# A graph layer's edge stages in a fixed order, its features and its router's ranks in batches

## The chip, the cores and the metric

The kernel runs on one core of one Trainium2 chip. The core has five engines with an instruction queue each: TensorE (PE, matrix products), VectorE (DVE), ScalarE (ACT), GpSimd (POOL; here it issues the indirect gathers) and SyncE (SP; here it only issues transfers). Each engine takes its instructions in order; they wait for each other by semaphores. The metric is device microseconds of one execution, the median of several.

## The reference

3125 nodes of 256 features and 53,125 edges (25,000 both ways, and one loop per node) pass four blocks, each added to its input after a layer norm. The names of the kernel's stages follow them.

```python
x = x + gnn0(layernorm(x), edge_index, edge_weight, ...)   # attention of four heads over the edges
x = x + moe0(layernorm(x), ...)                            # 16 experts, the best two of each node
x = x + gnn1(layernorm(x), src, dst, edge_type, ...)       # relations: 200 kinds of edges
x = x + ffn1(layernorm(x), ...)                            # only the rows with the highest router weight

# gnn0, per head:  w = exp(-relu((a_s[src] + a_d[dst] + aw_e * elem + ab) / 20))
#                  out = segment_sum(w * feats[dst], src) / segment_sum(w, src)
# gnn1:            alpha = exp(leaky_relu(h[src].w_src + h[dst].w_dst + rel_e.w_rel)); alpha / sum over its one column
#                  agg = segment_sum((h[src] + rel_e) @ Wn * alpha, dst); out = relu(agg) + loop_message
# ffn1:            weights = x @ wr + br; the kk best rows of each batch: gelu(x @ w1 + b1) @ w2 + b2, times weight
```

## The kernel before

The nodes stand in SBUF as 25 tiles of 128 rows (`self.x`). The edges of each graph layer are sorted on the chip by the node tile that receives them, so that each node tile is a bucket of 18 (the last has 8) edge tiles of 128 edges, 440 edge tiles in all. Up to six edge tiles make a group (`GRP`), which gives 74 groups in a layer.

The stages follow one another: the sort of layer 0's edges and layer 0's features; layer 0's edges (`heads_edges`); the experts and the combine of their results (`experts`); norms and features for layer 1 (`relations_features`); layer 1's edges (`relations_edges`); router and FFN (`depths`). The sort of layer 1's edges runs underneath: a generator `ranking` yields pieces of work that the edge loop of layer 0 draws one by one (`fill`), and its `move` steps run among the experts' row tiles.

For a group of edges the loop does this. GpSimd gathers a row of the feature table for each edge (L754, one indirect DMA per edge tile, into one of three `rows` buffers). SP loads the edges' other end, spread over all partitions, as `wide` (L744, one load per bucket, per kind of spread; layer 0 has one kind, layer 1 two). VectorE compares: `oh` (L762) is the one-hot of each edge's receiving node, `hot` (L771) that of the near rows as columns (one in layer 0, three in layer 1). TensorE multiplies `hot` with the near values into `ps_near` (L780), VectorE reduces it to `near` (L787). The weights follow: in layer 0 three VectorE steps `s` (L919 to L921) and two exponentials on ScalarE (L924, L925), then the message `rows` times weight (L926); in layer 1 `s` (L1310, L1279), the exponential (L1280), `s` again (L1281, L1282), a one-hot of the relation written behind the gathered row (L1313), and on ScalarE the one-hot of the node times the weight, `ohw` (L1319). TensorE adds it all up in PSUM, `ps_sums` (L798), over the tiles of a bucket. At a bucket's end VectorE adds what lay beyond the bucket's tiles, `more` (L804, a load on SP), giving `acc` (L806), and a `finish` function turns it into the node tile's new `x`. In layer 0 that also runs the gate in batches of node tiles (`gate`: norms, the experts' logits); in layer 1 it runs relation and loop products (`ps_rel`, `ps_loop`).

The order of these is only half written: `edge_stages` returns three stages, `gather` (with the comparisons), `message` and `add`, and `pipelined` calls them for groups one behind the other. The program runs under a scheduler, which places the instructions of each engine by its own estimates; that is the order in each queue.

After the experts, the combine gathers two result rows per node (L1170) and adds them to `x` (L1174). `relations_features` then loads its weights (`w3a`, `av`, L1198), takes their product (L1203), normalises all 25 tiles with one square root over them (`layer_norm("xn2")`, L157 to L163), and for each tile transposes it (`ps_x_t`), multiplies it by the weights (`ps_f`, L1264), copies it out and writes the table (L1270, five tiles a write).

`depths` starts behind layer 1's edges: weights loaded (L1375 on), all norms, the router weight of each row (`junk`, L1396, with `wc` as sums), a row of all weights on each partition (`wrow`, L1406 and L1410), and then the rank of each row as a count: for each of 25 tiles a comparison with all of `wrow` (`cmp`, L1426, in two pieces around the tile itself) and one for ties (`eq`, L1431). Rows whose rank is under `kk` get their weight as factor, and the FFN runs four tiles at a time (`ps_hid` L1453, `ps_out` L1464).

## Time and profile before

| | us |
|---|---|
| median of 3 runs (lowest to highest) | 2857.28 (2856.35 to 2861.86) |
| the profiled execution | 2845.15 |
| its span | 2842.8 |
| mean granted TensorE clock | 0.822 |

| engine | busy us | share of the span |
|---|---|---|
| TensorE | 1878.6 | 66% |
| VectorE | 1446.3 | 51% |
| GpSimd | 1167.4 | 41% |
| ScalarE | 390.7 | 14% |

The profile counts the busy time of each engine, and for the groups of instructions of one line the idle time of the engine in front of them, with the instruction that ended it. "issue" means that the engine waited for nothing that the profile shows, "remote" that what it waited for is not in the trace. The shares are means over stages with different limits; a stretch of the span has to be read by itself. Line numbers are those of the kernel printed above.

### The profile page before, as it was taken

Reading aid. Unit: us, or ns where it says so; the run is one execution under the profiler, and the core shown is the slowest. Engines: PE = TensorE matmul, PEld = TensorE weight load, DVE = VectorE, ACT = ScalarE, POOL = GpSimd, SP = SyncE. Lnnn points to the kernel's source line nnn. Section 1 sums busy time; section 2 is a strip of 40 time slices with the busy share of each in tenths; the row PEclk is TensorE's granted clock in tenths of the full one; section 3 lists DMA queues with packets and bytes.
Section 4 is the critical chain, followed back from the end, with each engine's and each line's share of the span. In section 5 each row is a group of like instructions: output and inputs, shape, how many; then the busy total and the mean of one; then the engine's idle time right before and its main releaser. Section 6 shows DMA issues by size and latency. Waiting matters only on the chain.

```text
span 2842.8 us, 24381 instructions
## 1 busy us (share of the span) xinstructions
PE 1878.6 (66%) x7534; PEld 1126.4 (40%) x7534; DVE 1446.3 (51%) x3397; ACT 390.7 (14%) x1097; POOL 1167.4 (41%) x1198
## 2 busy tenths in 40 slices
PE   3169554854544443399999991447878778785298
PEld 0024232543433332356666660323434334343166
DVE  4876225476665343644422224445655556549721
ACT  0000010010000000100112120112222222221012
POOL 4235306576654646034411115036666666650000
PEclk9999996676666667577799996768889888898599
DMA  2000325343444433144499982254545455431000
GB/s 83 0 3 5 104 89 137 93 130 112 115 100 114 116 100 101 49 150 130 131 316 318 317 291 84 87 156 131 148 129 148 130 142 149 128 85 34 8 21 18
DMA packets 258938, 334.04 MB, mean 118 GB/s; under 512 B 30861, under 2 KB 192407, under 8 KB 258807
## 3 DMA queue, kind: packets, MB, share of 16 engines
q1 hardware_dynamic: 197527, 191.26, 21.3%
q0 software_dynamic: 51920, 132.68, 17.6%
q10 hardware_dynamic: 9360, 8.52, 0.9%
q8 instruction: 61, 1.00, 0.1%
q14 instruction: 70, 0.57, 0.1%
HBM read 298.38 MB, written 33.98 MB: 117 GB/s over the span
## 4 chain that ended last, share of the span: by engine, by line
PE 39%; DVE 14%; issue 10%; POOL 9%; another core or an unknown queue 8%; DMA 4%; ACT 1%; SPq 0%; DVEq 0%; POOLq 0%; ACTq 0%
PE ps_sums L798 10%; PE ps_h L1130 9%; POOL rows L754 9%; PE ps_y L1147 4%; PE s_mv L560 3%; DVE cmp L1426 3%; PE ps_hid L1453 3%; PE ps_out L1464 3%; DMA rows<-table,s_idx 3%; DVE msg L926 2%; DVE hot L771 2%; PE ps_x_t L173 1%; PE ps_h_t L173 1%; PE ps_f L1264 1%
## 5 line engine op out<-in xcount | busy, mean ns | idle before, releaser
L754 POOL DMA_INDIRECT rows<-table,s_idx x880 | 848.6, 964 | 725.0 <-issue 240.4
L798 PE MATMUL ps_sums<-msg,oh 128*128 128x260 f32 x880 | 306.6, 519 | 261.8 <-DVE msg L926 143.1
L798 PE MATMUL ps_sums<-rows,ohw 128*128 128x457 f32 x880 | 414.0, 616 | 62.8 <-ACT ohw L1319 54.1
L798 PEld LDWEIGHTS ps_sums<-msg,oh 128*128 128x128 f32 x880 | 226.6, 265 | 325.1 <-issue 250.1
L560 PE MATMUL s_mv<-s_hv,s_hp 128*128 128x200 f16 (+1 forms) x832 | 246.8, 472 | 89.9 <-DVE s_hv L555 89.9
L798 PEld LDWEIGHTS ps_sums<-rows,ohw 128*128 128x128 f32 x880 | 179.0, 215 | 217.5 <-issue 149.6
L1130 PE MATMUL ps_h<-w,x_t 128*128 128x512 f32 x520 | 256.1, 638 | 0.0
L771 DVE TENSOR_SCALAR hot<-wide,pcols 128x768 bf16<-128x768 bf16 (+1 forms) x296 | 175.4, 597 | 73.9 <-PE ps_near L780 63.0
L560 PEld LDWEIGHTS <-s_hp 128*128 128x128 f16 x832 | 122.1, 147 | 208.7 <-issue 180.3
L762 DVE TENSOR_TENSOR oh<-ps_hold,s_row 128x768 f32<-128x768 f32 (+1 forms) x148 | 139.9, 946 | 125.7 <-remote 73.5
L1119 POOL DMA_INDIRECT xg<-xtab,who x65 | 61.9, 952 | 345.1 <-PE ps_x_t L173 302.6
L569 POOL DMA_INDIRECT s_tab<-s_rec,s_to x130 | 147.8, 1137 | 115.1 <-ACT s_rec L566 78.9
L780 PEld LDWEIGHTS <-hot 128*128 128x128 bf16 x1760 | 70.0, 98 | 212.3 <-issue 149.2
L1136 DVE TENSOR_TENSOR hid<-hid,ps_h 128x512 f32<-128x512 f32 x65 | 44.7, 688 | 210.3 <-ACT hid L1135 204.4
L1319 ACT ACTIVATE ohw<-oh,s 128x128 f32<-128x128 f32 x440 | 136.5, 388 | 106.6 <-DVE s L1282 75.2
L1130 PEld LDWEIGHTS ps_h<-w,x_t 128*128 128x128 f32 x520 | 102.8, 209 | 105.7 <-issue 105.5
L926 DVE TENSOR_TENSOR msg<-rows,ps_hold 128x1536 f32<-128x1536 f32 x74 | 128.1, 1731 | 2.0 <-ACT ps_hold L924 1.9
L787 DVE TENSOR_REDUCE near<-ps_near 128x24 f32<-128x72 f32 (+2 forms) x148 | 29.4, 198 | 190.3 <-remote 150.2
L1147 PE MATMUL ps_y<-w,h_t 128*128 128x256 f32 x520 | 122.9, 379 | 0.7 <-ACT h_t L175 0.7
L1147 PEld LDWEIGHTS ps_y<-w,h_t 128*128 128x128 f32 x520 | 98.7, 190 | 41.7 <-issue 30.6
L545 DVE TENSOR_TENSOR s_hp<-num_p,s_pp 128x1024 f16<-128x1024 f16 x104 | 71.8, 690 | 82.8 <-PE s_mv L560 81.4
L1313 DVE TENSOR_TENSOR rows<-ps_hold,s_val 128x1200 f32<-128x1200 f32 x74 | 101.1, 1367 | 6.1 <-PE ps_sums L798 6.1
(307 smaller groups left out, 2344.2 us busy)
## 6 DMA issues: line engine op xcount, KB each, us to landing
w<-in_L_ffn_w_dram SPq DMA_DIRECT2D x195, 512.0 KB
wide<-s_w SPq DMA_DIRECT2D x72, 576.0 KB
rows<-table,s_idx POOLq DMA_INDIRECT x880
ytab<-y ACTq DMA_DIRECT2D x65, 128.0 KB
sums<-sums_z SPq DMA_DIRECT2D x5, 1142.5 KB
more<-sums SPq DMA_DIRECT2D x25, 228.5 KB
sums<-sums_z SPq DMA_DIRECT2D x5, 650.0 KB
table<-f SPq DMA_DIRECT2D x5, 650.0 KB
```

Source lines behind the costliest of these rows:

```text
L560: nc.tensor.matmul(ps[:, : NK * V], hp[:, :, j], rec[:, :, :, j].rearrange("p k v -> p (k v)"), start=(j0 + j == 0), stop=(j0 + j == C - 1),)
L569: d = nc.gpsimd.indirect_dma_start(out=tab, out_offset=bass.IndirectOffsetOnAxis(ap=to[:, i : i + 1], axis=0), in_=out[:, k * CH * V : (k ...
L754: nc.gpsimd.indirect_dma_start(out=rows[:, j, :width], out_offset=None, in_=table, in_offset=bass.IndirectOffsetOnAxis(ap=st["idx"][:, k + ...
L762: nc.vector.tensor_tensor(oh[:, :n, :], numbers[:, None, :P].to_broadcast(sh), st["row"][:, k : k + n, None].to_broadcast(sh), op=OP.is_equal,
L771: nc.vector.tensor_scalar(t[:, : n // 2, :], w, at, None, op0=OP.is_equal)
L798: nc.tensor.matmul(ps[:, :W], oh[:, j, :], msg[:, j, :], start=(head and j == 0), stop=(last and j == n - 1),)
L926: nc.vector.tensor_tensor(msg[:, :n, :HO].rearrange("p j (h o) -> p j h o", o=O), rows[:, :n, :HO].rearrange("p j (h o) -> p j h o", o=O), ...
L1130: nc.tensor.matmul(ph[:, i * HID : (i + 1) * HID], xt[:, c, :], w12[:, i, c, :], start=(c == 0), stop=(c == C - 1),)
L1147: nc.tensor.matmul(py[:, :D], ht[:, c, :], w3[:, c, :], start=(c == 0), stop=(c == HC - 1))
L1313: nc.vector.tensor_tensor(rows[:, :n, R0:], self.numbers[:, None, :R].to_broadcast(sh), st["val"][:, k : k + n, None].to_broadcast(sh), op ...
L1319: nc.scalar.activation(ow[:, j, :], oh[:, j, :], AF.Copy, scale=s[:, 1, j : j + 1])
L1426: nc.vector.tensor_scalar(cmp[:, s:e], wrow[:, s:e], w, None, op0=op, op1=OP.add, accum_out=rank[:, t, i : i + 1],)
```

## The change

- Both edge stages run in an order that is written out and that the scheduler leaves alone (`edges`, under `manual_schedule`). In each step: the spread of the group two ahead (now one `wide` load per group and kind, four buffers; `more` with the bucket's first), the gathers of group g, its comparisons and its near products on TensorE, in layer 1 the relation's one-hot, then weights, message and sums of group g-1, then the near reduction of group g, one piece of `fill`, and the end of a bucket for group g-2.
- `relations_features` is a generator. Its weights are prepared before the experts; the norms and features of layer 1 follow the combine in batches of node tiles (ends 4, 8, 12, 16, 20, 22, 25).
- The router of the last block, but for the FFN itself, leaves `depths`. Its weights are loaded ahead of layer 1's edges; norms, router weights and counts run in batches in the `finish` of layer 1's edges (ends 5, 10, 15, 20, 23, 25). A batch counts its new columns for the old tiles, and all columns so far for the new ones, into further columns of `rank`; `depths` adds them up.

```diff
-    def edge_stages(self, pool, st, table, width, into, near, others, messages, W, sums, finish):
+    def edges(
+        self, pool, st, table, width, into, near, others, messages, W, sums, finish,
+        fill=(), prepare=None,
+    ):
...
+        def spread(g):
+            b, k, n = groups[g][:3]
+            wide[g] = []
+            for i, w in enumerate(st["wide"]):
+                t = pool.tile([P, G // 2, 2 * P + 8], BF16, name=f"wide{i}", bufs=4)
+                src = w[k : k + n, :].rearrange("(o k i) p -> o k (i p)", o=1, i=2)
+                nc.sync.dma_start(t[:, : n // 2, : 2 * P], src.to_broadcast([P, n // 2, 2 * P]))
+                wide[g].append(t[:, : n // 2, : 2 * P])
+            if groups[g][3]:
+                more[b] = pool.tile([P, W], F32, name="more")
+                nc.sync.dma_start(more[b], sums[b])
...
+        with tc.manual_schedule():
+            spread(0)
+            spread(1)
+            for g in range(len(groups) + 2):
+                if g + 2 < len(groups):
+                    spread(g + 2)
+                if g < len(groups):
+                    rows = gather(g)
+                    oh, pe = hots(g)
+                    if prepare:
+                        prepare(*groups[g][1:3], rows)
+                if 0 <= g - 1 < len(groups):
+                    message(g - 1)
+                if g < len(groups):
+                    live[g] = rows, oh, picked(g, pe)
+                    if g > 0:
+                        next(fill, None)
+                if 0 <= g - 2:
+                    close(g - 2)
+            for _ in fill:
+                pass
...
-    def experts(self, fill):
+    def experts(self, fill, done):
...
                         self.x[:, t, :], yg, top[i][:, t : t + 1], self.x[:, t, :],
                         op0=OP.mult, op1=OP.add,
                     )
+                done(t)
...
-            self.h1 = self.layer_norm("xn2")
+            self.h1 = self.normed("xn2")
...
+            ends = list(range(4, NT - 4, 4)) + [NT - 3, NT]
+            def done(b):
+                if b + 1 not in ends:
+                    return
+                i = ends.index(b + 1)
+                t0, t1 = ends[i - 1] if i else 0, b + 1
+                self.norm_tiles(self.h1, t0, t1)
...
+        def route(b):
+            if b + 1 not in ends:
+                return
+            i = ends.index(b + 1)
+            t0, t1 = ends[i - 1] if i else 0, b + 1
+            self.norm_tiles(z, t0, t1)
+            for t in range(t0, t1):
+                junk = pool.tile([P, D], F32, name="junk")
+                nc.vector.scalar_tensor_tensor(
+                    junk, z[:, t, :], 1.0, wr, op0=OP.mult, op1=OP.mult,
+                    accum_out=wc[:, t : t + 1],
+                )
...
+            end = min(N, t1 * P)
+            for t in range(t0):
+                count(t, t0 * P, end, OP.is_gt, 3 + i)
+            for t in range(t0, t1):
+                lo, hi = t * P, min(N, (t + 1) * P)
+                count(t, 0, lo, OP.is_ge, 0)
+                count(t, lo, end, OP.is_gt, 1)
...
-                    self.experts([lambda f=f: f(moves) for f in steps])
-        self.relations_features()
-        self.relations_edges(load())
-        self.depths()
+                    self.experts([lambda f=f: f(moves) for f in steps], next(features))
+                    next(features, None)
+        st = load()
+        with tc.tile_pool(name="route", bufs=1) as pool:
+            self.router(pool)
+            self.relations_edges(st)
+            self.depths()
```

## The prediction

> **What bounds the kernel now.** I cut the span at its stage borders first, since shares over the whole of it mix different limits. This is the busy time of each engine by stretch: layer 0's edges, experts, combine and layer 1's features, layer 1's edges, the router, the last FFN.
>
> ```profile
> core 0: us, PE busy (x) PEld busy (x) DVE busy (x) ACT busy (x) POOL busy (x), PEclk, DMA share, GB/s
> 434.00:1170.00 736.00, 384.19 (x1586) 282.81 (x1586) 406.83 (x958) 51.54 (x190) 429.28 (x437) 0.68 0.40 108
> 1170.00:1714.00 544.00, 507.55 (x1904) 320.97 (x1904) 204.75 (x447) 87.71 (x165) 131.85 (x132) 0.87 0.68 221
> 1714.00:1892.00 178.00, 46.08 (x245) 32.96 (x245) 78.18 (x219) 12.16 (x29) 63.66 (x67) 0.66 0.35 109
> 1892.00:2565.00 673.00, 528.34 (x2449) 266.08 (x2449) 372.67 (x947) 172.95 (x591) 399.92 (x424) 0.87 0.49 131
> 2565.00:2683.00 118.00, 35.68 (x139) 25.50 (x140) 115.08 (x238) 12.21 (x20) 0.25 (x1) 0.65 0.06 20
> 2683.00:2842.80 159.80, 151.81 (x562) 101.95 (x562) 30.52 (x69) 35.73 (x59) 0.00 (x0) 0.98 0.06 20
> ```
>
> Experts and the last FFN are TensorE's. The router is VectorE's alone (115 of 118 us). In the two edge stages no engine is busy throughout, so the next view is what their costly groups wait for (layer 0's stretch):
>
> ```profile
> L754 POOL DMA_INDIRECT rows<-table,s_idx x437 | 429.4, 983 | 295.2 <-DVE msg L926 161.5 <-issue 122.5 <-DVE r L937 6.7
> L762 DVE TENSOR_TENSOR oh<-ps_hold,s_row 128x768 f32<-128x768 f32 (+1 forms) x73 | 69.0, 945 | 99.2 <-remote 73.5 <-PE ps_sums L798 16.7 <-issue 9.0
> L787 DVE TENSOR_REDUCE near<-ps_near 128x24 f32<-128x72 f32 x74 | 16.8, 227 | 78.7 <-remote 38.7 <-PE ps_near L780 35.5 <-issue 4.5
> L806 DVE TENSOR_TENSOR acc<-ps_sums,more 128x260 f32<-128x260 f32 x25 | 10.6, 425 | 84.2 <-remote 70.8 <-PE ps_sums L798 10.1 <-issue 3.1
> ```
>
> A gather takes 0.95 us plus 0.30 us of issue, so one every 1.25 us: 440 of them need 550 us. The stage takes 736, and the difference of 186 is almost the waits marked "remote" (73.5 + 38.7 + 70.8 = 183), whose releaser the trace does not see. One of them, from the timeline:
>
> ```profile
> 820.40 1.75 DVE L926 TENSOR_TENSOR msg<-rows,ps_hold 128x1536 f32<-128x1536 f32 x1
> ...
> 829.85 0.94 POOL L754 DMA_INDIRECT rows<-table,s_idx  x1 [0.30 <-issue]
> 834.72 0.43 DVE L806 TENSOR_TENSOR acc<-ps_sums,more 128x260 f32<-128x260 f32 x1 [12.57 <-remote]
> 835.30 1.21 PE L798 MATMUL ps_sums<-msg,oh 128*128 128x260 f32 x2 [16.11 <-DVE acc L806]
> ```
>
> VectorE stands 12.57 us in front of the bucket's sum, TensorE stands with it, and GpSimd issues gathers until its three row buffers are full. Layer 1 has the same sight at every bucket, where its near reduction waits (105.8 us "remote" over the stage):
>
> ```profile
> 2123.09 0.18 DVE L787 TENSOR_REDUCE near<-ps_near 128x6 f32<-128x18 f32 x1 [4.54 <-remote]
> 2123.50 0.94 POOL L754 DMA_INDIRECT rows<-table,s_idx  x1 [2.80 <-PE ps_near L780]
> 2123.84 0.61 DVE L771 TENSOR_SCALAR hot<-wide,pcols 128x768 bf16<-128x768 bf16 x1
> 2124.43 0.61 DVE L771 TENSOR_SCALAR hot<-wide,pcols 128x768 bf16<-128x768 bf16 x1
> 2124.75 0.95 POOL L754 DMA_INDIRECT rows<-table,s_idx  x1 [0.30 <-issue]
> ```
>
> **The change part by part.** Sums go against the profiled execution, 2845.15 us (span 2842.8 and 2.35 outside); the median of the runs is 2857.28, so 12.1 us are added at the end.
>
> *The router leaves the tail.* Before, 118 us lie between the last edge result (2565) and the last FFN (2683): 25 normalisations 8.2 us, 25 junk products 8.7, 49 comparisons 88.9, 25 ties 7.8, small reads 8.9, and starts. After, five batches of five, five, five, five and three tiles run inside layer 1's edges; two tiles remain. For these: two normalisations and products about 3 us, transposes and the copy about 2, 23 short comparisons of 181 columns (2 tiles, cut at node 3125). The nearest row is the tie over 128 columns, 0.35 us, plus 0.09 us for the accumulator's read: 23 x 0.44 = 10; two long comparisons 1.9 each and ties: 5. Together 20 us. Gain 98, between 90 and 105.
>
> *Features follow the expert results.* From the last combine to layer 1's first gather it is 1789.9 to 1870.9, 81 us: the `av` load 9.1 us, `w3a` products and weights to 1811.7, then 25 tiles at a pitch of 1.87 us to 1858, the table's write 4.4, the sort's load 8.1. After, only the last batch of three stands there: normalisation about 3, 3 x 1.87 = 5.6, write 4.4, load 8.1, slack 2: 23 us. Gain 58 (40 to 65). The other batches lie in the combine, which goes by GpSimd at 2 x 1.25 = 2.5 us a tile; VectorE needs per tile 2 x 0.44 + 0.6 + 0.33 + 0.43 = 2.2 and TensorE 1.87. It is covered, narrowly; without that cover 23 tiles cost what they did, 43 us. The weights' preparation (1790 to 1811, 21 us) moves ahead of the experts, where VectorE, ScalarE and TensorE are in a chain on the logits: 0 to 21, I take 5, since its loads have no predecessor. The router's two 1 MB weight loads now precede layer 1's on SP's queue; at the 343 GB/s that these loads reached around 2572 us that is 6 us; I take 5 (0 to 10).
>
> *Sort moves.* Fourteen VectorE instructions of layer 1's sort (at 898 to 905) went among layer 0's edges and go back to the experts: 7 us of an engine busy 205 of 544 there: nothing; without that cover 7.
>
> *Layer 0's edges.* Now every group issues in a set order: its gathers, its comparisons, TensorE's near products ahead of the sums of the group before, that group's message, only then the near reduction. So VectorE no longer stands directly behind `ps_near`: it has the message (s 0.5, exp 0.4, product 1.75) to do. The near reduction's waits on PE (35.5) should go. The remote waits are unexplained, hence bounds: all stay, 736; all go, 550 and about 26 for the first landing and the tail, 576. Against it: the ranking piece and the gate's batches now stand in order on VectorE. A ranking piece is 2.5 us (0.38 + 0.2 + 1.02 + 0.59 + 0.59 overlapping) in a group whose other work is 4.2 us: 6.7 of 7.5, covered. A gate batch of five tiles holds VectorE for normalisation 5 x 0.6 + 5 x 0.41 + 1.6 (root and its table load, 1.28) and then TensorE's 5 x 2.0 us of transposes and logits (the pitch at 1173.5 to 1175.5) before the logits can be added: some 17 us, in which GpSimd runs on for at most a group or so, 7.5. Behind the logits' add the next comparisons wait, and TensorE for them. Five batches x 9 = 45. Of the 183 us of remote waits I let a third through, 60, because GpSimd is one group ahead and the mean wait is 183/23 = 8 us. 550 + 20 + 45 + 60 = 675: gain 61, between 0 and 160. The wide copies go from one load per bucket to one per group (74 and 148 issues at 0.37 us on SP): SP is idle otherwise; its four buffers reach two groups (15 us) ahead and one such load landed in 8 us at three times the size.
>
> *Layer 1's edges.* From first gather to 2565 it is 694. VectorE's 373 plus 97 moved from the router is 470, TensorE 528, gathers 550. The wait of the near reduction again falls behind the message. A router batch is 97/5 = 19 us during which VectorE makes no comparisons and, past the buffers' slack, everything stands: 5 x (19 - 7.5) = 58; the chain product, copy, comparison adds about 2 each, 10. After such a pause TensorE's sums take 7.00 instead of 4.85 us (2098.73 and 2106.01 of this trace): 5 x 2.15 = 11. TensorE's own pause of about 3 us per bucket is half covered: 25 x 1.5 = 38. 550 + 20 + 58 + 10 + 11 + 38 = 687: gain 7; from 80 less to 80 more.
>
> One rule speaks against the whole gain in the edges. The four lines at 2123.50 to 2124.75 show gathers still 1.25 us apart while VectorE runs the wide comparison in bf16. The Trainium skill, "SBUF — State Buffer", section "Who interferes with whom", says that a `tensor_scalar` in a two-port mode takes the port pair that GpSimd needs for its descriptors, and that the other then blocks altogether. By it, 296 comparisons of 0.6 us would add up to 178 us once gathers set the pace, and the forecast would be 2,815. The trace shows no such lengthening, so the sum has none.
>
> Sum: -98 - 58 + 10 + 0 - 61 - 7 = -214. 2845 - 214 = 2631, and 12 for the median: 2643; I say **2640**.
>
> **The rivals.**
> (1) Both edge stages run at the gathers' pace: the waits came from the old order, in which VectorE stood in front of a result just asked for. For it: 736 - 183 is 553, exactly the gathers. Against it: TensorE is idle too, so the order may not be their cause. Layer 0 at 550 + 20 + 45 = 615, layer 1 at 550 + 20 + 58 = 628: 2640 - 60 - 59 = 2520.
> (2) The waits stay and the batches come on top: layer 0 at 736, layer 1 at 694 + 58 + 21 = 773. For it: the waits' releaser is not in the program's order. 2640 + 61 + 86 = 2787. Still faster, as router and features alone gain 146 net.
> (3) Slower: the order closes the row buffers' loop. A buffer is held from the first gather (7.5 us) over landing (2.5), the next group's comparisons and one-hot (4.1), weights (2.9), near products and sums (7.5), 24.5 us at best; three buffers give 8.2 us a group. If each hand-over between engines waits for the previous group's, in place of overlapping it, one more step of 7 to 10 us joins: at 33 us it is 11 us a group. Both stages together took 1430 us for 148 groups, 9.66 a group; with 146 gained elsewhere the kernel is slower from 1576/148 = 10.65 a group, a hold of 32 us. At 11.3 us: 2857 - 146 + 148 x 1.64 = 2954. For it: layer 1's stalls already reach GpSimd through its buffers (2.80 us, line 2123.50). Against it: the new order asks for each result one step earlier than it uses it.
>
> **How the numbers follow.** Likeliest case 0.52, rival 1 0.25, rival 2 0.13, rival 3 0.10. Its own range is 2570 to 2710. To leave out no more than two in ten, the range reaches to rival 1 below and to the low side of rival 2 above, 2500 to 2765; the unknown costs (160 in layer 0, 80 either way in layer 1) would reach as far. About 0.2% (5.7 us) can be told from no change: faster 0.90, within 0.01, slower 0.09.
>
> **What would show it.** After the last edge, about 20 us to the last FFN's first transposes; some 23 us from the last combine to the first gather of layer 1; 440 gathers in about 675 us in layer 0 and 690 in layer 1, with "remote" in front of the near reduction well below 106 us in layer 1; gathers standing some 9 us at each of ten batches. Wrong if "remote" keeps its 183 us in layer 0, if gathers come slower than 1.25 us apart inside a group, or if each group's row buffer is held over 30 us.

## The result, and the profile after

| | us |
|---|---|
| changed kernel, median of 4 runs (lowest to highest) | 3274.1 (3265.8 to 3274.6) |
| kernel before, beside it, median of 4 runs | 2859.6 (2856.4 to 2892.0) |
| ratio | 1.141 [1.133, 1.150] |
| span of the profiled execution, before and after | 2842.8, 3272.3 |
| granted TensorE clock, before and after | 0.822, 0.768 |

The change costs 14% where the forecast was a gain of 7.6% (2640 to 2857). The busy time by stretch of the changed kernel: layer 0's edges, the features' preparation, experts, combine with features, layer 1's edges, the rest of the router, the last FFN.

```profile
core 0: us, PE busy (x) PEld busy (x) DVE busy (x) ACT busy (x) POOL busy (x), PEclk, DMA share, GB/s
428.70:1274.00 845.30, 393.30 (x1586) 287.21 (x1586) 453.99 (x968) 51.29 (x190) 427.48 (x440) 0.67 0.35 96
1274.00:1333.00 59.00, 18.76 (x93) 15.27 (x94) 42.56 (x144) 7.55 (x22) 4.54 (x6) 0.50 0.39 137
1333.00:1834.00 501.00, 495.86 (x1845) 311.45 (x1844) 172.19 (x343) 81.60 (x144) 127.48 (x127) 0.91 0.71 231
1834.00:1956.00 122.00, 64.96 (x163) 41.80 (x163) 54.03 (x173) 11.09 (x32) 47.99 (x51) 0.50 0.33 101
1956.00:3070.00 1114.00, 619.13 (x2511) 304.70 (x2511) 519.28 (x1272) 192.65 (x611) 416.98 (x440) 0.71 0.31 84
3070.00:3092.00 22.00, 16.25 (x38) 8.02 (x39) 13.99 (x62) 7.37 (x12) 0.00 (x0) 0.77 0.00 0
3092.00:3272.00 180.00, 171.88 (x651) 117.29 (x649) 42.31 (x93) 39.67 (x65) 0.00 (x0) 0.99 0.05 18
```

With the borders set by events (first gather, last `acc`, first `ps_h`, first and last result gather, first `ps_hid`) the stages of the two profiled executions are:

| stage | before | after | difference |
|---|---|---|---|
| layer 0's edges | 740 | 845 | +105 |
| to the experts' first product | 49 | 60 | +11 |
| experts | 500 | 501 | +1 |
| combine (with features, after) | 66 | 81 | +14 |
| to layer 1's first gather | 86 | 41 | -45 |
| layer 1's edges | 688 | 1114 | +426 |
| router's rest and last FFN | 284 | 202 | -82 |

The loss lies in the edge stages: +531 us, and in layer 1 most of it. No engine does more there than 619 of 1114 us. What the groups of layer 1's stretch wait for (busy time, mean ns of one, then the idle time before and what ended it):

```profile
L763 POOL DMA_INDIRECT rows<-table,s_idx x440 | 417.0, 948 | 688.5 <-PE ps_sums L813 497.1 <-issue 119.5 <-remote 61.1
L1446 DVE TENSOR_SCALAR_CACHE_REDUCE cmp<-wrow,wc 128x640 bf16<-128x640 f32 (+13 forms) x95 | 90.6, 954 | 12.1 <-ACT wrow L1472 9.5
L1392 DVE SCALAR_TENSOR_TENSOR x<-ps_loop,has,x 128x256 f32<-128x256 f32 x48 | 23.2, 484 | 86.2 <-issue 77.6 <-PE ps_loop L1380 7.7
L822 DVE TENSOR_TENSOR acc<-ps_sums,more 128x457 f32<-128x457 f32 x25 | 15.9, 635 | 100.3 <-remote 91.8 <-PE ps_sums L813 8.5
L801 DVE TENSOR_REDUCE near<-ps_near 128x6 f32<-128x18 f32 x74 | 12.8, 174 | 271.2 <-remote 182.0 <-PE ps_near L790 80.1 <-PE ps_sums L813 9.2
L1386 DVE TENSOR_TENSOR agg<-acc,ps_rel 128x256 f32<-128x256 f32 x24 | 10.1, 421 | 77.4 <-PE ps_rel L1373 69.6 <-remote 7.8
```

The same groups in the kernel before:

```profile
L754 POOL DMA_INDIRECT rows<-table,s_idx x440 | 416.0, 945 | 343.5 <-issue 117.3 <-DVE near1p L651 85.4 <-PE ps_sums L798 73.8
L1355 DVE SCALAR_TENSOR_TENSOR x<-ps_loop,has,x 128x256 f32<-128x256 f32 x50 | 24.0, 480 | 69.3 <-PE ps_sums L798 52.0 <-issue 8.6 <-PE ps_loop L1343 6.0
L806 DVE TENSOR_TENSOR acc<-ps_sums,more 128x457 f32<-128x457 f32 x25 | 15.9, 635 | 18.0 <-PE ps_sums L798 9.8 <-issue 8.2
L787 DVE TENSOR_REDUCE near<-ps_near 128x6 f32<-128x18 f32 x74 | 12.6, 170 | 111.6 <-remote 111.6
L1349 DVE TENSOR_TENSOR agg<-acc,ps_rel 128x256 f32<-128x256 f32 x25 | 10.3, 413 | 7.2 <-PE ps_rel L1336 4.5 <-issue 2.7
```

GpSimd stands 497 us because TensorE's sums have not given a row buffer back; before, that wait was 74 us. VectorE stands 535 us in front of four instructions, `near`, `acc`, `agg` and `x`; before, 206. Three of them are the end of a bucket. Here is one such end in the timeline (start, duration, idle time in front and what ended it):

```profile
2548.93 0.19 PE L790 MATMUL ps_near<-rel_p,hot 128*128 128x3 bf16 x2
2549.50 4.88 PE L813 MATMUL ps_sums<-rows,ohw 128*128 128x457 f32 x12 [0.30 <-issue]
...
2556.79 0.18 DVE L801 TENSOR_REDUCE near<-ps_near 128x6 f32<-128x18 f32 x1 [7.78 <-remote]
2557.68 0.95 POOL L763 DMA_INDIRECT rows<-table,s_idx  x1 [0.30 <-issue]
2561.19 0.64 DVE L822 TENSOR_TENSOR acc<-ps_sums,more 128x457 f32<-128x457 f32 x1 [4.22 <-remote]
2561.42 0.95 POOL L763 DMA_INDIRECT rows<-table,s_idx  x1 [2.80 <-remote]
...
2564.89 0.42 DVE L1386 TENSOR_TENSOR agg<-acc,ps_rel 128x256 f32<-128x256 f32 x1 [3.07 <-PE ps_rel L1373]
...
2569.57 1.00 DVE L1392 SCALAR_TENSOR_TENSOR x<-ps_loop,has,x 128x256 f32<-128x256 f32 x2 [3.66 <-issue]
2570.49 1.64 DVE L777 TENSOR_SCALAR hot<-wide,pcols 128x768 bf16<-128x768 bf16 x3
...
2575.79 7.71 PE L813 MATMUL ps_sums<-rows,ohw 128*128 128x457 f32 x12 [3.02 <-ACT ohw L1356]
```

Two things are to be seen. First, the end of a bucket stands in VectorE's queue as a ladder: `acc`, then TensorE's `ps_cnt` and `ps_rel`, then `agg`, then TensorE's `ps_loop`, then `x`; only behind `x` come the comparisons of the next group (2570.49), and TensorE's next sums start at 2575.79, 26 us after the start of the last (2549.50). Second, the "remote" waits are not gone. The near products are recorded as done by 2549.2 and the sums by 2554.4, yet `near` starts at 2556.79 and `acc` at 2561.19. The trace's semaphore events have an update by TensorE at 2556.76, right in front of `near`, and the last of a burst at 2561.16, right in front of `acc`. Layer 0 has the same at its buckets' ends:

```profile
1192.17 0.29 PE L790 MATMUL ps_near<-near0p,hot 128*128 128x12 bf16 x6
1194.00 2.87 PE L813 MATMUL ps_sums<-msg,oh 128*128 128x260 f32 x12 [1.53 <-DVE msg L949]
1201.53 0.23 DVE L801 TENSOR_REDUCE near<-ps_near 128x24 f32<-128x72 f32 x1 [7.68 <-remote]
1210.04 0.43 DVE L822 TENSOR_TENSOR acc<-ps_sums,more 128x260 f32<-128x260 f32 x1 [8.28 <-remote]
```

The sums end at 1196.87 by their records, and VectorE gets them at 1210.04. I call this TensorE's late signals. Over layer 0 they make 128 us in front of `near` and 118 in front of `acc`; before, all of layer 0's were 183.

The distance from one `acc` to the next puts a size on the router's batches. In layer 1 it was 27.2 to 27.4 us at almost every bucket before; after, it is 38.1 to 39.9 at a plain bucket, and 55.7, 64.5, 80.2, 79.8 and 63.7 where a router batch stands: 5 x 39.1 less than their sum is 148 us.

### The profile page after: what moved, and what is told of

Same layout as the page of the kernel before. It is cut to its first block, busy times and chain, and to the rows that moved or that the text cites. A ratio compares the mean times of both kernels' runs of the same rounds, so it can differ in the third digit from the quotient of the medians.

```text
span 3272.3 us, 24762 instructions
## 1 busy us (share of the span) xinstructions
PE 2005.0 (61%) x7534; PEld 1182.0 (36%) x7534; DVE 1532.3 (47%) x3561; ACT 409.6 (13%) x1121; POOL 1163.6 (36%) x1198
## 5 line engine op out<-in xcount | busy, mean ns | idle before, releaser
L777 DVE TENSOR_SCALAR hot<-wide,pcols 128x768 bf16<-128x768 bf16 (+1 forms) x296 | 165.1, 600 | 5.6 <-DMA wide<-s_w 5.6
L790 PE MATMUL ps_near<-near0p,hot 128*128 128x12 bf16 x440 | 22.9, 172 | 204.5 <-DVE hot L777 186.1
L1356 ACT ACTIVATE ohw<-oh,s 128x128 f32<-128x128 f32 x440 | 136.6, 389 | 33.9 <-DVE s L1317 23.3
L822 DVE TENSOR_TENSOR acc<-ps_sums,more 128x260 f32<-128x260 f32 (+1 forms) x50 | 26.6, 531 | 233.7 <-remote 209.9
L790 PE MATMUL ps_near<-near1p,hot 128*128 128x3 bf16 x440 | 42.9, 166 | 148.4 <-DVE hot L777 141.8
L1367 PE MATMUL ps_cnt<-ident,acc 128*128 128x128 f32 (+1 forms) x50 | 22.1, 441 | 180.4 <-DVE acc L822 171.5
```

Of the source, the lines that this page charges most:

```text
L777: nc.vector.tensor_scalar(t[:, : n // 2, :], wide[g][min(i, 1)], at, None, op0=OP.is_equal)
L790: nc.tensor.matmul(pe[:, j * 3 * nv : (j + 1) * 3 * nv], t[:, j // 2, j % 2 * P : (j % 2 + 1) * P], v.rearrange("p q v -> p (q v)"), start ...
L1356: nc.scalar.activation(ow[:, j, :], oh[:, j, :], AF.Copy, scale=s[:, 1, j : j + 1])
```

## The experiments

Four chips took part, here A to D, each with runs of the kernel before: A 2870.5 (median of 12, 2852.8 to 2925.0; 2904.2 in the single run beside the first four kernels), B 2844.3, C 2634.7, D 2637.0. The difference between A, B and C, D matters below. "Layer 0" and "layer 1" are the stages of the table above, 740 and 688 us before, 845 and 1114 after. A diff without another remark is against the changed kernel.

### Which part costs it (chip A)

**The scheduler orders the same instructions.**

```diff
-        with tc.manual_schedule():
+        if True:
```

> The new edge loops as they are written, but the scheduler may again reorder them (the manual order is lifted); batches of features and of the router stay. Theory A (the fixed order itself costs: it puts each bucket's finish, with four round trips between VectorE, TensorE and ScalarE, and the router's batches bare into VectorE's queue): layer 1's edges fall from 1114 us to about 780 (688 of before and most of the router's 100), layer 0's from 845 to 740, in all about 2830. Rival B (the smaller spread loads or the near products ahead of the sums cost, not the order): stays above 3150.

Measured: 2901.0; layer 0 754, layer 1 833. Against the 845 and 1114 of the first comparison, which ran on another chip, some 370 us of the loss go with the fixed order alone. With the scheduler the kernel is level with the single run of the one before beside it (2904.2), and 1% over the median of twelve on that chip (2870.5). The forecast of 2830 was too low.

**The ranks behind the edges.**

```diff
-                self.route(t)
...
+            for t in range(NT):
+                self.route(t)
```

> The router's batches all run behind layer 1's edges instead of in their finish; the rest is the changed kernel. If the batches stand bare in the loop and cost their full length there, layer 1's edges lose some 110 to 140 us (1114 to about 990) and the stretch to the FFN gains 90 to 105, so the time is 3230 to 3270. If the batches are what breaks the loop (they hold comparisons, so buffers and signals), layer 1 falls to 750 and the time to about 3000.

Measured: 3198.7; layer 1 975 (-139), tail and FFN 265 (+63). What moves behind the edges here is the comparisons, 96 us of VectorE; norms and router products still lie among the edges (19 us). The comparisons cost 139 us among the edges and 63 behind them, so they stand in the edges at more than their full length. The time came out below both forecasts.

**The bucket's end ahead of the next group's message.** `close(g - 2)` is called before `message(g - 1)`.

```diff
+                if 0 <= g - 2:
+                    close(g - 2)
                 if 0 <= g - 1 < len(groups):
                     message(g - 1)
...
-                if 0 <= g - 2:
-                    close(g - 2)
```

> The end of a bucket is written ahead of the next group's message instead of behind the near reduction. In the changed kernel the bucket's sum waits for a TensorE count that includes the next bucket's first six sums. If that wait is a cost of its own, the remote waits in front of acc (210 us in both layers) go and the time falls by 100 to 200, to 3070 to 3170. If the delay only moves (the near reduction then waits for the same late signal), it stays within 60 of 3272.

Measured: 3163.7; layer 1 1026 (-89), and "remote" in front of `acc` falls from 92 to 7 us in layer 1. `acc` had waited for more than its own sums: both halves of `ps_sums` are one tile, and in the program `acc` stands behind the six sums of the next bucket's first group (on chip D, below, it starts 0.04 us after these end). In front of `near` the 182 us stay. In layer 0 the same move leaves 96 of 118 us in front of `acc`, and the stage falls by 23 us only.

**Features alone, under the scheduler** (the first two diffs together; the loops' new text and the spread loads by group remain).

> The scheduler's order in both edge stages and the router's batches behind the edges: of the change only the features behind the combine, the weights prepared early and the spread by groups are left. If the router's batches cost layer 1 as much as they save behind it, this is 40 to 90 us below e1's 2901 on the same chip and 0.5 to 2 per cent under the kernel before (features -31, prepared weights +11). If the batches were worth moving, it stands above e1.

Measured: 2902.1, ratio 1.012 [1.009, 1.016]; layer 1 770, tail and FFN 265. Against the first run, layer 1 is 63 us shorter and the tail 64 longer: under the scheduler too the router in batches is worth nothing. And layer 1 is still 82 us over its 688, while VectorE's "remote" waits there grew by 115 (to 211 us in front of `near`, 112 before).

**A better fixed order:** `acc` and TensorE's relation and loop products behind the old group, VectorE's `agg` and `x` one step later, ranks late.

```diff
+                if rest:
+                    rest()
+                rest = None
+                begun = close(g - 2) if 0 <= g - 2 else None
                 if 0 <= g - 1 < len(groups):
                     message(g - 1)
...
+                if begun:
+                    rest = begun()
```

> Fixed order, bucket sums ahead of the next message, TensorE's part of a finish behind the message, VectorE's part of it a step later behind the next comparisons; router behind the edges. If the finish's round trips bare in VectorE's queue are what is left of the fixed order's price, layer 1's edges fall from 1026 (sums first) less 139 (ranks late) to about 780, and the kernel to about 2950. If the late signals set the pace whatever stands in the queue, layer 1 stays above 870 and the kernel above 3030.

Measured: 3025.4; layer 0 792, layer 1 854. With each round trip behind other work layer 1 loses 121 us against the late ranks alone (975), but stays 166 over the kernel before, with 208 us "remote" in front of `near`. That lies between the two forecasts.

### The late signals (chips A and B)

**Half the gathers.** The odd groups' rows are a zero tile, so their edges are left out; the others have two row buffers.

```diff
+        fixed = pool.tile([P, G, into], F32, name="fixed", bufs=1)
+        nc.vector.memset(fixed, 0.0)
...
-            rows = pool.tile([P, G, into], F32, name="rows", bufs=3)
+            if g % 2:
+                return fixed
+            rows = pool.tile([P, G, into], F32, name="rows", bufs=2)
```

> Every second group gathers nothing: its rows are a tile of zeros, so the results of those edges are left out; two row buffers in place of three. TensorE, VectorE and ScalarE work as before. Theory C (TensorE's signals come late while gathers flow): the remote waits, 520 us in both edge stages, fall by more than half, and the kernel to below 2950. Rival D (they come from TensorE's own stream of short instructions or from the order of waits): they stay above 400 and the kernel above 3150.

Measured: 2933.7; layer 0 644, layer 1 979, "remote" 27 us in all. With half the gathers and two buffers the late signals are gone; and layer 1 is slow without them too, so they are not all of its loss.

**The near products twice** (`for j in list(range(n)) * 2`).

> The changed kernel with every near product issued twice on TensorE (same result), which by the trace costs at most 0.45 us more a group where TensorE is not late. Theory C2 (while gathers flow, TensorE's instructions complete one by one at about 0.7 us, however short they are): each late near reduction waits for 6 (layer 0) or up to 18 (layer 1) more of them, 4 to 12 us, and the remote waits in front of near rise from 320 us in both layers to 500 or more; the kernel to 3450 to 3700. Rival D2 (the delay is a span set by the gathers alone): remote stays at 500 to 560 and the kernel below 3340.

Measured: 3349.0; layer 0 892, with 281 us "remote" in front of `near` and 13 of `acc`; layer 1 1144, with 35, 33 and 25 in front of `near`, `acc` and `agg`. Between the two forecasts. In layer 0 the lateness moved from `acc` to `near`. In layer 1 `near` waits as long as in the changed kernel (267 us, there 271), but the trace puts 228 of it down to `ps_sums` now. The stages grew by 47 and 30 us; the lateness does not simply grow with the number of small products.

**One near product per edge tile in layer 1, not three** (`picks = [near[:, b]]`), which leaves the relation's part out of the score.

> The changed kernel without the two relation products per edge tile in layer 1's near values, so that the relation's part of the score is left out: 6 near products a group in place of 18, all else the same. Theory C2: layer 1's near reductions wait 12 x 0.7 = 8.4 us less where they were late by 7.6, so their 182 us of remote waits fall below 40, and layer 1's edges lose 100 to 200 us. Rival D2: the remote waits of layer 1 stay within 40 us of 274 (near and acc), the stage loses no more than 40.

Measured: 3313.5; layer 1 1153, not shorter. "Remote" in front of `near` is gone, but 145 us stand in front of `acc` and 151 in front of `agg`. That reads as if the waits had a place in time, and whatever comes next in VectorE's queue met them. The forecast was right on `near` and missed on the stage.

**Plain loads in place of the odd groups' gathers**, of as many bytes out of the table's first tiles, on SP (chip B; three row buffers). A group's rows are asked for ahead of the spread loads here.

```diff
+            if g % 2:
+                nc.sync.dma_start(
+                    rows[:, :n, :width], table[: n * P, :].rearrange("(j p) c -> p j c", p=P)[:, :, :width]
+                )
+                return rows
...
+                if g < len(groups):
+                    rows = gather(g)
                 if g + 2 < len(groups):
                     spread(g + 2)
                 if g < len(groups):
-                    rows = gather(g)
```

> The changed kernel, where every second group's rows come by one plain load on SP of as many rows and bytes out of the table's first tiles, in place of six gathers of GpSimd (so those edges take the wrong rows). The bytes moved are those of the changed kernel. If GpSimd's gathers are what makes TensorE's signals late, the remote waits fall as with half the gathers, below 150 us in both stages. If the bytes or packets that land in SBUF do it, they stay above 350.

Measured: 2852.3; layer 0 642, layer 1 902, "remote" 4 us. With the bytes kept and half of GpSimd's indirect DMAs gone the signals are in time. So the late signals go with these gathers, not with the bytes.

**Two row buffers in the changed kernel** (chip B, `bufs=2`).

> The changed kernel with two row buffers in place of three, every group gathered: the control for the run with half the gathers, which had two buffers as well. If the gathers cause the late signals, the remote waits stay above 350 us in both edge stages (544 with three buffers, 27 with half the gathers) and the kernel at 3250 or more. If it was GpSimd's lead of three buffers, they fall below 150 here too.

Measured: 3219.7; layer 0 845 with 193 us "remote", layer 1 1063 with 3. It was meant to part two explanations, the gathers and GpSimd's lead, and one layer went each way.

The start times of the gathers in the traces say what the layers differ in: how many gathers follow each other without a pause, 0.30 us from one to the next. In layer 1 most of them come twelve at a time in the kernel before and in the changed one, and six at a time with two buffers, with half the gathers and with plain loads. The late signals are there with runs of twelve and not with runs of six. In layer 0 two buffers still leave runs of 18, and 193 us "remote". In layer 1 TensorE's late updates end in a burst, and it comes 2.3 to 2.4 us after the last gather of the run (2557.68 and 2561.16 above), as a median of each kernel: before, changed, better order, spread loads alone. The burst's distance from the last matmul's recorded end differs between these four: 2.9, 6.6, 3.4 and 6.8 us. So on these chips the signals seem to wait for the end of a long run of gathers. This is a reading of the traces and not shown by a run made for it; a run also ends where a row buffer is missing, which waits for the same signals.

**The spread loads by group alone**, put into the kernel before (chip B; diff against that).

```diff
...
-                now[b] = [spread(i, b) for i in range(len(st["wide"]))]
+            for at in (0, 1, 2) if g == 0 else (g + 2,):
+                spread(at)
...
```

> The kernel before with one part of the change: one spread load per group, four buffers, two groups ahead, in place of one per bucket. If the small spread loads are what makes the scheduled loop slower than before (features only: layer 1's edges 770 in place of 688 us), layer 1 comes near 770 and the kernel 2 to 3 per cent above the one before. If it is the order in which the new text gives the near products and the one-hots to the scheduler, this stays within 1 per cent of the kernel before.

Measured: 2923.4, ratio 1.026 [1.023, 1.030]; layer 1 759. The line that pays, in the groups of its layer 1 stretch:

```profile
L773 DVE TENSOR_SCALAR hot<-wide,pcols 128x768 bf16<-128x768 bf16 (+1 forms) x222 | 132.0, 598 | 211.0 <-remote 190.9 <-PE ps_sums L800 11.4 <-PE ps_near L782 5.2
```

The comparisons write buffers that TensorE has read, and in front of them stand 191 us whose releaser the trace does not show; with the kernel's own loads such waits stood in front of `near`, 112 us.

### The part that gains, and chips without late signals (B, C and D)

**Only the features of the change**, in the kernel before: `experts` calls `done(t)`, the weights are prepared before it, everything else as it was (chip B; the same kernel again on D).

```diff
...
+                done(t)
...
+                features = self.relations_features()
                 with tc.tile_pool(name="move1", bufs=1) as moves:
-                    self.experts([lambda f=f: f(moves) for f in steps])
-        self.relations_features()
+                    self.experts([lambda f=f: f(moves) for f in steps], next(features))
+                    next(features, None)
```

> The kernel before, edge loops and router untouched, with the features behind the combine and their weights prepared ahead of the experts. From the changed kernel's trace: combine and features 152.4 to 121.4 us, the stretch in front of the experts 48.8 to 59.6. So 20 us, 0.7 per cent, faster than before; if the preparation can be hidden no better and the features' weights take SBUF or queue time from the edges, 0 to 0.3.

> The kernel before with the features behind the combine (0.9877 on a chip with late signals). It moves nothing in the edge loops, so its gain, 30 to 35 us, should be the same without late signals: 0.985 to 0.992.

Measured: 2810.3 on B, ratio 0.988 [0.985, 0.990]; 2592.3 on D, ratio 0.983 [0.980, 0.985]. It beats both kernels, by somewhat more than forecast. From the last result gather to layer 1's first gather it takes 30.7 us, 86 before.

**Two row buffers under the scheduler** (chip C), with the features: in layer 1 (`bufs=2 if others else 3`), in both layers (`bufs=2`), and in the better fixed order.

> The kernel before with the features behind the combine, and two row buffers in place of three in layer 1 alone, in the scheduler's order. If GpSimd's lead of three groups is what makes TensorE's signals late there (none were late in the fixed order with two buffers), the 104 us of remote waits in layer 1 fall below 30, its edges from 687 to 620 to 660 and the kernel to 2740 to 2785. If two buffers leave GpSimd idle as long as the late signals did, it stays at 2800 to 2830 or gets slower, with few remote waits.

> As the run before, with two row buffers in both layers. Layer 0 had 193 us of remote waits even with two buffers in the fixed order, so if the lead alone decides nothing there, layer 0 stays at 730 to 790; if it does, its remote waits (196) halve and the stage falls to 650 to 700.

> The fixed order with sums first, the finish split and the ranks behind the edges (layer 1's edges 854 us, 208 of them remote waits), with two row buffers. If the late signals were the rest of the fixed order's excess over the scheduler's, layer 1 falls to 700 to 760. If the order's own chain at a bucket's end holds it, it stays at 800 or more with no remote waits.

Measured: 2741.3, ratio 1.040 [1.037, 1.042]; 2788.3; 2845.7, where the kernel before takes 2634.7. Layer 1 takes 773 in the first, and 635 on D with three buffers (the kernel before agrees on C and D within 0.1%). This chip shows no "remote" wait at all, so the runs could not tell what they were for; they do say that the third buffer is worth some 138 us of layer 1 and 47 of layer 0 (597 in the first run, 644 in the second). And they compare the orders with two buffers, ranks late in both and no late signals: layer 1 takes 771 in the scheduler's order and 825 in the better fixed one, which still loses 54 us.

**The changed kernel where signals are in time** (chip D).

> The changed kernel unchanged, once more. The last three runs stood on a chip where the kernel before took 2635 us instead of 2840 to 2900 and no run showed a remote wait, so the late signals belong to the chip, not to the program alone. If this call's chip shows none, the changed kernel loses its 520 us of remote waits, but in layer 1 other waits take part of their place (with two buffers it was 1063 without any): 2850 to 2980, 8 to 13 per cent over the kernel before there. If it shows them, 3220 to 3280 against 2840 to 2900. A ratio near 1 without late signals would mean that they alone made the change slow.

Measured: 2864.5, ratio 1.086 [1.083, 1.089], and not one "remote" wait; layer 0 670, layer 1 899, against 595 and 635 in the kernel with the features alone. Its groups in layer 1's stretch:

```profile
L763 POOL DMA_INDIRECT rows<-table,s_idx x432 | 412.0, 954 | 457.8 <-PE ps_sums L813 340.7 <-issue 111.9 <-DMA rows<-table,s_idx 2.7
L1392 DVE SCALAR_TENSOR_TENSOR x<-ps_loop,has,x 128x256 f32<-128x256 f32 x50 | 24.2, 484 | 63.9 <-PE ps_loop L1380 63.0
L822 DVE TENSOR_TENSOR acc<-ps_sums,more 128x457 f32<-128x457 f32 x25 | 15.9, 635 | 122.6 <-PE ps_sums L813 122.6
L801 DVE TENSOR_REDUCE near<-ps_near 128x6 f32<-128x18 f32 x74 | 12.8, 173 | 81.9 <-PE ps_near L790 81.9
L1386 DVE TENSOR_TENSOR agg<-acc,ps_rel 128x256 f32<-128x256 f32 x25 | 10.5, 421 | 53.3 <-PE ps_rel L1373 53.3
```

And the same in the kernel with the features alone, on that chip:

```profile
L754 POOL DMA_INDIRECT rows<-table,s_idx x440 | 417.4, 949 | 235.2 <-issue 119.2 <-PE ps_sums L798 65.8 <-DVE near1t L652 29.8
L1367 DVE SCALAR_TENSOR_TENSOR x<-ps_loop,has,x 128x256 f32<-128x256 f32 x48 | 23.1, 482 | 56.8 <-PE ps_loop L1355 56.8
L806 DVE TENSOR_TENSOR acc<-ps_sums,more 128x457 f32<-128x457 f32 x25 | 15.7, 628 | 2.6 <-PE ps_sums L798 2.6
L787 DVE TENSOR_REDUCE near<-ps_near 128x6 f32<-128x18 f32 x74 | 12.5, 169 | 0.0
L1361 DVE TENSOR_TENSOR agg<-acc,ps_rel 128x256 f32<-128x256 f32 x24 | 10.1, 420 | 9.2 <-PE ps_rel L1348 8.5
```

The four waits are 322 us in the written order and 69 in the scheduler's. One end of a bucket in the changed kernel (the view ends at 2046, before the third comparison):

```profile
2031.89 0.18 DVE L801 TENSOR_REDUCE near<-ps_near 128x6 f32<-128x18 f32 x1 [0.23 <-PE ps_near L790]
2032.14 4.88 PE L813 MATMUL ps_sums<-rows,ohw 128*128 128x457 f32 x12 [0.30 <-ACT ohw L1356]
...
2037.06 0.63 DVE L822 TENSOR_TENSOR acc<-ps_sums,more 128x457 f32<-128x457 f32 x1 [5.00 <-PE ps_sums L813]
...
2039.82 0.42 DVE L1386 TENSOR_TENSOR agg<-acc,ps_rel 128x256 f32<-128x256 f32 x1 [2.13 <-PE ps_rel L1373]
...
2044.09 1.00 DVE L1392 SCALAR_TENSOR_TENSOR x<-ps_loop,has,x 128x256 f32<-128x256 f32 x2 [3.18 <-PE ps_loop L1380]
2045.01 1.12 DVE L777 TENSOR_SCALAR hot<-wide,pcols 128x768 bf16<-128x768 bf16 x2
```

Each wait now has its releaser in the trace, and the ladder is bare: 5.00 for the next bucket's six sums, 2.13 for the relation product, 3.18 for the loop product, with the next comparisons behind all three. The distance from `acc` to `acc` is 28.8 to 30.8 us at a plain bucket and 47.9, 57.1, 62.6, 71.9 and 61.1 with a router batch; in the kernel with the features alone it is 23.3 to 27.2. The loss of 264 in layer 1 divides into about 147 for the batches (their sum less 5 x 30.7) and 117 for the order, some 5 us at each of the 23 full distances. So of the 426 us on the first chip some 160 go with the late signals there. The run with plain loads agrees: layer 1 takes 902 us on B without them, 899 here.

**The spread loads by group again** (chip D).

> The kernel before with the spread loads by groups (2.6 per cent slower, layer 1's edges 759 in place of 688, with 191 us of remote waits in front of the comparisons). If the late signals were the whole of that loss, it is within 1 per cent of the kernel before on a chip without them; if the smaller loads cost by themselves, 2 per cent or more remain.

Measured: 2630.7, layer 1 622: no cost there. What they cost on B was the late signals alone.

## Why the prediction was wrong

**Layer 1's edges, "gain 7; from 80 less to 80 more", came out as +426.** This is the step that failed, by three of its terms.

- *The bucket's end.* It was put at "TensorE's own pause of about 3 us per bucket is half covered", 38 us, with the argument that "the new order asks for each result one step earlier than it uses it". For the near reduction that was not enough: it waits 81.9 us on D, 0.0 in the old order, as TensorE has the sums of an older group in front of its products. And it does not hold for `close` at all, which asks for `acc`, `agg` and `x` one directly behind another. The pause that counts is VectorE's, and it is the whole ladder: on D 10.3 us idle in the end shown. Moving the bucket's end ahead of the next message took 89 us off, and the better order 121 beyond the ranks.
- *The batches.* "5 x (19 - 7.5) = 58" gave each a slack of 7.5 us. The term has two faults. VectorE's work in them is 113 us and not 97, and no slack is seen: they cost 148 by the distances, and their comparisons alone 139 by the run with the ranks late. A batch grows from 16 to 41 us with its comparisons, and it stands at the bottom of the ladder, where the row buffers' lead is already used up.
- *The waits.* The sum began at the gathers' 550 us and had no term for "remote" in layer 1, though before had 106 us of it there. After, the fixed order has 274 in front of `near` and `acc`; where there are none, the stage loses 264 in place of 426.

What took the place of the forecast is the mechanism of the third rival, which had a chance of 0.10: the row buffers' loop is closed, GpSimd waits 497 us for sums (on D 341, against 66 in the old order). It set its deciding point at 10.65 us a group; the stages took (845 + 1114) / 148 = 13.2. Its price, 2954, was too low: it had one more hand-over in each group, and neither the batches nor the late signals. On D the stages took 10.6 us a group where the kernel with the features alone took 8.3.

**Layer 0's edges, "gain 61, between 0 and 160", came out as +105.** "I let a third through, 60" was a guess about a wait without an explanation. All of it stayed and grew, from 183 to 246 us, since `near` and `acc` now stand where the late signals are. The gate's batches, put at 45, cost 14.3 each by the distances of `acc` (45.7 against 31.4, at four of the five), so about 72. On D, where the waits are absent, the stage takes 670, near the forecast of 675, which is luck: the stage of the old order takes 595 there, so it is a loss there as well. Where the waits are absent, the old order already runs near the gathers' 550 us (595 and 635), and an order had little to win back.

**The router, -98, measured -82** (284 to 202): right in kind. The stretch between edges and FFN is 22 us, as forecast; but the FFN's own stretch has 651 matrix products against 562 and takes 180 us against 160, as part of them had lain beside the old router. As the batches cost 139 us or more in the edges, the move as a whole loses.

**The features, -58 + 10, measured -45 + 14 + 11 = -20** in this kernel and 1.2% and 1.7% alone. The border to layer 1's gathers takes 41 us from the last result gather, 31 with the features alone; forecast were 23 from the last combine, which lies 5 us later, and 5 for the router's loads in front; the combine was "covered, narrowly" and lengthened from 66 to 81 us on the chips with late signals, and on D from 61 (in the run with the spread loads alone) to 69; the preparation took 11 of the bounds 0 to 21.

**The sort's moves, 0**: the experts stay at 501 us.

**The rule on ports**, which the forecast left out of its sum. Gathers of the changed kernel beside three comparisons, on GpSimd and VectorE:

```profile
2543.90 0.95 POOL L763 DMA_INDIRECT rows<-table,s_idx  x1 [13.85 <-PE ps_sums L813]
2544.19 1.64 DVE L777 TENSOR_SCALAR hot<-wide,pcols 128x768 bf16<-128x768 bf16 x3
2545.15 0.95 POOL L763 DMA_INDIRECT rows<-table,s_idx  x1 [0.30 <-issue]
2546.40 0.95 POOL L763 DMA_INDIRECT rows<-table,s_idx  x1 [0.30 <-issue]
```

They start 1.25 us apart, as 392 of the 439 distances in layer 1 do, and no gather of that stage takes over 0.96 us. What holds them is the 13.85 us for a row buffer. In layer 0 the forecast's "no such lengthening" is not quite so: 34 of 440 gathers take 1.0 to 1.6 us there, 10 us too much in all, beside several kinds of VectorE instruction. Whether the comparisons ran in a two-port mode no trace here tells. (The price of 2,815 should be 2818 by its own terms, 2640 and 178.)

**Named as what would show it wrong**: "if "remote" keeps its 183 us in layer 0", and "if each group's row buffer is held over 30 us". Both came true: the first with 246 us, the second with 40 us by three buffers at 13.2 us a group.

## What to carry to other kernels

An order written by hand must put other work behind every question to another engine, the ends of loops included; before trusting one, list for each engine what its queue holds between a request and its use, and what the awaited count takes in (here the halves of one tile, six products too many). Work moved into a stage is hidden only by the slack that the buffers still have at that place, not by an engine's idle share. And a wait that the trace can't explain is not to be counted as a gain: ask first whether it is there on another chip.

## What was not expected of the hardware

The kernel before takes 2838 to 2925 us on chips A and B and 2632 to 2644 on C and D, with no "remote" wait on the latter in any kernel run there. On A, B and the chip of the first comparison TensorE's signals come late. In layer 1 of the changed kernel they come at the same place of each bucket, first 0.7 us or a small multiple of it apart (0.72, 1.39 to 1.42, 2.80 to 2.82) and then the rest in a burst, 0.04 us apart. In the two ends shown `near` and `acc` start 7 to 13 us behind the recorded ends of their matmuls. Half the indirect gathers ends it (27 and 4 us), as do runs of six gathers in place of twelve in layer 1 (3 us); yet on D runs of 18 and more bring no late signal. The traces of the chips with late signals also lack some of TensorE's updates (125 of 1440 in the changed kernel, none on D), so a single step can't be assigned to a single product. What is slow, the products or only their signals, can't be told, as the profile models the ends of matmuls; why the chips differ stays open; and that the spread loads move the late signals to another instruction was seen, but not why they make them longer.

TensorE's sums behind a pause ran slower: the twelve passes of a group take 4.88 us at 2549.50, in a flow, and 7.71 at 2575.79, and the granted clock in layer 1's stretch is 0.71 after and 0.87 before. The Trainium skill, "TensorE: Matmul & The Clock Gate", Part 1, has the clock at half after an idle stretch and full again after sustained work. Both numbers agree with that.
